# Softmax maxima over partitions in a graph attention kernel: from TensorE transposes to VectorE block transposes

## The chip, the cores and the metric

The kernel runs on one core of one Trainium2 chip. The core has five engines that run their own instruction queues side by side and meet by semaphores: TensorE (PE, matrix products and transposes, results in PSUM), VectorE (DVE), ScalarE (ACT), GpSimd (POOL) and SyncE (SP, which issues most DMAs). The metric is the device time of one execution in microseconds; the number given for a kernel is the median of its runs.

## The reference

The input is x of 3327 rows and 512 columns, and adj, a 3327 x 3327 matrix of zeros and ones. Two graph attention layers come first, then a layer norm, then a layer with signs and a second layer norm:

```python
def _gat_layer(x, W, adj):
    proj = x @ W
    Wh, Ws = jnp.split(proj, 2, axis=-1)
    scores = Wh @ Ws.T
    a = jax.nn.softmax(scores, axis=-1) * adj
    out = a @ Wh
    out = out + x
    return jax.nn.leaky_relu(out, NEG_SLOPE)
...
x = _layernorm(x + gat2(x, adj), axis=-1)
bw = sign(weight); ba = maximum(sign(x), 0)
x = _layernorm(x + relu(adj @ (ba @ bw.T)), axis=-1)
```

The change touches the softmax alone: each row of scores needs its maximum, which is subtracted before the exponential.

## The kernel before

The kernel works in 26 tiles of 128 rows. For each of the two attention layers (`attention(l, att)`) the scores are made transposed: the keys j lie on the 128 partitions, and the query rows i along the free axis. So the softmax's maximum over j is a maximum over partitions and over tiles. The rows i are taken in halves of 256 (`g`, 13 of them) and in chunks `c` of two halves (7 chunks; the last, c=6, has one half). `q` runs over 13 pairs of key tiles.

The products use a seven-product scheme (Strassen's, in Winograd's form) on 128x256 f32 blocks. For one (c, q), `scores` issues in two steps: the products z1, x2, z6, y5 in the first, z7, y3, z4 in the second. They accumulate in three PSUM banks, Z, X and Y (pool `ps_ch`). ScalarE copies p1, u2, p5, u3 and c21 out of them (L599, L634), VectorE adds c11 (`add11`, L609), c22 (`add22`, L624) and c12 (`add12`, L630). A bank is used again as soon as it is read out: the next z1 goes into the bank that `add11` has emptied, the next x2 into the one that `add12` has emptied.

`maximum` (L652) folds the scores of each q into `top[g]`, an array of 128 partitions x 2 x 256. After the last q of a chunk, `column_max` makes from it `off[g]`, in which every partition holds the maxima of the 256 columns. Its three parts are placed in one step: `fold` at -0.04 (takes the maximum of the two 256-wide parts of `top`), `across` at 0.36, `back` at 0.9. The numbers are places in the order of the step: all work of one step is sorted by its number, and each engine takes its instructions in that order.

The step loop (L976 to L1019) is one hand-written order for all engines. In step v it issues, for the half and q of number v+3, `shift` (0.0, subtract `off`, L727, VectorE) and `exponential` (0.12, L730, ScalarE); for number v+2 `running` (0.01, the sums, L738) and `masked` (0.4, times adj, L743, VectorE, followed by four sums on POOL, L781 to L784); in every second step, and in some more, `halved_sums` (0.6, L763, VectorE), `halved` (0.61, the casts L749 and L750, ScalarE) and `exact` (0.62, L772), with `keep_blocks` in the following step at 0.5: POOL stores the fp8 block `ab` to `adj_d` (L766). The tile `ab` has two buffers, so a third block waits for the landing of the store before last. For number v+30, counted in steps of `scores`, it issues the products of a later chunk, and `values` (L808) for number v. So `across` and `back` of chunk c are issued while the attention of chunk c-1 ends and the scores of chunk c+1 begin; the first `shift` that needs the new `off` is the first of the step after `back`.

`across` before: TensorE transposes 128x128 blocks of `top` into PSUM (`ptop`, L684, four a chunk), VectorE takes the row maxima (L687) and repeats them over 128 columns by multiplying a tile of ones (L689). `back` transposes these again (`poff`, L694), and VectorE copies the result to `off` (L698). Both PSUM tiles are of the pool `ps_tr`, which has one buffer that `finish` also uses (L848, L894, L904).

Of the kernel before, what the change touches and what calls it, by code (L numbers as in the profile page):

```python
# [9 lines left out]
F32 = mybir.dt.float32  # L10
# [5 lines left out]
ALU = mybir.AluOpType  # L16
AX = mybir.AxisListType
PSUM = bass.MemoryType.PSUM

P = 128  # L20
CT = 4
CW = CT * P
B = 32
HW = CW // 2
# [6 lines left out]
def kernel(  # L31
# [8 lines left out]
    nc = tc.nc  # L40
# [12 lines left out]
    def tiles_of(c):  # L53
        return range(c * CT, min(NT, (c + 1) * CT))

    def halves_of(c):
        return [g for g in (2 * c, 2 * c + 1) if g < NQ]
# [9 lines left out]
    keep = ctx.enter_context(tc.tile_pool(name="keep", bufs=1))  # L67
    ring = ctx.enter_context(tc.tile_pool(name="ring", bufs=2))
    ops = ctx.enter_context(tc.tile_pool(name="ops", bufs=2))
    small = ctx.enter_context(tc.tile_pool(name="small", bufs=4))  # L70
    ps_ch = ctx.enter_context(tc.tile_pool(name="ps_ch", bufs=3, space=PSUM))
    ps_acc = ctx.enter_context(tc.tile_pool(name="ps_acc", bufs=4, space=PSUM))
    ps_tr = ctx.enter_context(tc.tile_pool(name="ps_tr", bufs=1, space=PSUM))
# [7 lines left out]
    ident = keep.tile([P, P], F32, name="ident")  # L81
    make_identity(nc, ident)
    ident_h = keep.tile([P, P], BF16, name="ident_h")
    nc.vector.tensor_copy(ident_h, ident)
    ones = keep.tile([P, P], F32, name="ones")
    nc.vector.memset(ones, 1.0)
    eps = keep.tile([P, 1], F32, name="eps")
    nc.vector.memset(eps, EPS)
    mv = keep.tile([P, NT, 2], F32, name="mv")
# [461 lines left out]
    def attention(l, att):  # L551
# [5 lines left out]
        sc, top, total, off, adj, acc, gs, xs, ch = ({} for _ in range(9))  # L557
# [29 lines left out]
        def scores(c, q, s):  # L587
# [66 lines left out]
            if s == 1:  # L654

                after.append((-0.05, lambda: maximum(mine[0])))
                if q == NQ - 1:
                    after.extend(column_max(c))
# [8 lines left out]

        def column_max(c):

            n = len(tiles_of(c))  # L670
            mx = small.tile([P, CT], F32, tag="mx", name=f"mx_{l}_{c}")
            rep = [top[g][:, 1, ts(a, P)] for g in halves_of(c) for a in range(2)]

            def fold():
                for g in halves_of(c):
                    nc.vector.tensor_tensor(
                        top[g][:, 0], top[g][:, 0], top[g][:, 1], ALU.max
                    )

            def across():  # L680
                pt = ps_tr.tile([P, CT, P], F32, tag="tr", name=f"ptop_{l}_{c}")
                for i, g in enumerate(halves_of(c)):
                    for a in range(2):
                        nc.tensor.transpose(  # L684
                            pt[:, 2 * i + a, :], top[g][:, 0, ts(a, P)], ident
                        )
                nc.vector.reduce_max(mx[:, :n], pt[:, :n, :], axis=AX.X)  # L687
                for a in range(n):
                    nc.vector.tensor_scalar(rep[a], ones, mx[:, a : a + 1], None, ALU.mult)  # L689

            def back():
                pb = ps_tr.tile([P, CW], F32, tag="tr", name=f"poff_{l}_{c}")
                for a in range(n):
                    nc.tensor.transpose(pb[:, ts(a, P)], rep[a], ident)  # L694
                for i, g in enumerate(halves_of(c)):
                    off[g] = att.tile([P, 1, HW], F32, tag=f"off{i}", bufs=1,
                                      name=f"off_{l}_{g}")
                    nc.vector.tensor_copy(off[g][:, 0], pb[:, ts(i, HW)])  # L698

            return [(-0.04, fold), (0.36, across), (0.9, back)]  # L700

        def load_adj(g, q):
# [235 lines left out]
        else:  # L938
# [16 lines left out]
            n = len(steps) - end - 2  # L955
# [11 lines left out]
        mine = [i for i, e in enumerate(steps) if e[1] % L == l]  # L967
# [8 lines left out]
        for v in range(-LOOK - 4, len(steps)):  # L976
            u = v + LOOK
# [7 lines left out]
            for lead, load in ((2, load_xs), (4, load_gs)):  # L985
                if 0 <= u + lead < len(ahead):
                    c, q, h = ahead[u + lead]
# [23 lines left out]
            if last and 0 <= v - first_products < EARLY:  # L1011
                p = v - first_products
# [314 lines left out]
```

## Time and profile before

| what | value |
|---|---|
| median of 3 runs | 2633.66 us (2631.25 to 2634.98) |
| profiled execution | 2629.29 us |
| its span in the trace | 2627.5 us |
| mean granted TensorE clock | 0.998 |
| first and last `fold` (L676) | 267.7 and 2418.7 us |
| `fold`, 26 instructions | 10.0 us busy, 421 ns each |
| `shift` (L727), 338 instructions | 247.1 us busy, 731 ns each |
| `masked` (L743), 338 instructions | 237.5 us busy, 703 ns each |
| POOL waiting at L781 for L743 | 720.1 us in 260 waits |
| ScalarE's exponential waiting for L727 | 362.5 us in 218 waits |
| HBM traffic over the span | 242 GB/s |

The profile is of one execution. "Busy" is the time in which an engine's instructions overlap the clock, a share of the span; TensorE's instructions overlap each other, so their spacing says more than their own lengths. In a group's line, "idle before" is how long the engine stood still just before the instructions of that group, and after the arrow stands who ended that. There are 14 places at which `column_max` runs, 7 a layer, about 155 us apart in the middle of a layer: near 268, 416, 575, 734, 894, 1052 and 1177 us in layer 0, and 1487, 1636, 1800, 1964, 2127, 2291 and 2419 us in layer 1. Before the first of each layer there are no `values` yet, so TensorE does scores alone; after the last there are no scores any more.

### The profile page before, as it was taken

The page shows a single profiled execution, that of the slowest core. Times are in us where ns is not written, and L with a number is a line of the kernel's source. Part 1 is how long each engine was busy: PE and PEld are TensorE (multiplying, and loading weights), DVE is VectorE, ACT ScalarE, POOL GpSimd, SP SyncE. Part 2 cuts the span into 40 slices and gives each one's busy share as a digit, 9 for nine tenths or more (in the row PEclk, how much of TensorE's full clock was granted, in tenths as well). Part 3 has the DMA queues.
Part 4 walks back from the last instruction along what each step waited for, and adds up shares of the span by engine and source line. Part 5 has one row for each costly group of instructions (what it writes and reads, how often), then busy time and mean ns, then how long its engine had stood idle before and what let it go on. Part 6 is the DMA issues. An engine that isn't in the chain of part 4 may idle for free. (4 is left out here: it accounts for less than half of the span.)

```text
span 2627.5 us, 40294 instructions
## 1 busy us (share of the span) xinstructions
PE 2594.9 (99%) x12656; PEld 2249.1 (86%) x12656; DVE 2089.6 (80%) x4279; ACT 788.1 (30%) x1954; POOL 1098.4 (42%) x2025
## 2 busy tenths in 40 slices
PE   9999999999999999999999999999999999999998
PEld 6888888888888888887888888888888888888787
DVE  5864888889898886677875689888898888767976
ACT  2323332333333332222232333333333333222143
POOL 2640344444444444546552134444444444455510
PEclk9999999999999999999999999999999999999999
DMA  6855777787777776797865678777777777677775
GB/s 202 297 196 177 241 239 266 239 275 253 264 243 244 263 245 222 237 256 243 295 235 182 226 229 277 248 236 266 240 275 249 236 267 238 223 262 257 265 246 176
DMA packets 308055, 639.17 MB, mean 243 GB/s; under 512 B 34855, under 2 KB 175745, under 8 KB 306298
## 3 DMA queue, kind: packets, MB, share of 16 engines
q1 hardware_dynamic: 272140, 530.29, 61.9%
q0 software_dynamic: 35664, 106.18, 11.0%
q8 instruction: 104, 1.70, 0.3%
q14 instruction: 117, 0.96, 0.1%
q10 hardware_dynamic: 30, 0.03, 0.0%
HBM read 529.69 MB, written 106.67 MB: 242 GB/s over the span
## 5 line engine op out<-in xcount | busy, mean ns | idle before, releaser
L582 PE MATMUL pZ<-gs,xs 128*128 128x256 f32 x2496 | 636.0, 379 | 1.3 <-ACT u L599 1.3
L781 POOL TENSOR_TENSOR as<-s 128x128 f32<-128x128 f32 x338 | 162.4, 480 | 1048.1 <-DVE s L743 720.1
L582 PEld LDWEIGHTS pZ<-gs,xs 128*128 128x128 f32 x2496 | 473.5, 190 | 66.7 <-ACT u L599 2.4
L808 PE MATMUL acc<-ws,s 128*128 128x256 f32 x1352 | 402.2, 379 | 0.0
L808 PE MATMUL acc<-wh,s 128*128 128x256 f32 x1352 | 355.7, 379 | 0.6 <-DVE s L743 0.4
L808 PE MATMUL acc<-ws,as 128*128 128x256 f32 x1352 | 349.8, 380 | 3.9 <-POOL as L783 3.6
L730 ACT ACTIVATE s<-s 128x512 f32<-128x512 f32 x338 | 213.4, 631 | 362.8 <-DVE s L727 362.5
L582 PE MATMUL pY<-gs,xs 128*128 128x256 f32 x1248 | 320.8, 379 | 1.4 <-ACT p L599 1.4
L808 PEld LDWEIGHTS acc<-ws,as 128*128 128x128 f32 x1352 | 255.1, 190 | 44.6 <-POOL as L783 5.7
L808 PEld LDWEIGHTS acc<-wh,s 128*128 128x128 f32 x1352 | 256.6, 190 | 36.3 <-DVE s L743 1.5
L808 PEld LDWEIGHTS acc<-ws,s 128*128 128x128 f32 x1352 | 255.1, 190 | 33.9
L652 DVE TENSOR_TENSOR top<-top,s 128x512 f32<-128x512 f32 x312 | 223.7, 730 | 71.6 <-ACT s L639 51.8
L582 PEld LDWEIGHTS pY<-gs,xs 128*128 128x128 f32 x1248 | 236.6, 190 | 35.4 <-ACT p L599 3.3
L727 DVE TENSOR_TENSOR s<-s,off 128x512 f32<-128x512 f32 x338 | 247.1, 731 | 0.1
L743 DVE TENSOR_TENSOR s<-s,adj 128x512 f32<-128x512 f32 x338 | 237.5, 703 | 9.5 <-DMA adj<-in_adjT_dram 0.7
L738 DVE TENSOR_TENSOR total<-total,s 128x512 f32<-128x512 f32 x312 | 232.3, 745 | 0.0
L599 ACT COPY u<-pZ 128x256 f32<-128x256 f32 x312 | 115.8, 371 | 347.2 <-PE pZ L582 345.6
L783 POOL TENSOR_TENSOR as<-s 128x128 f32<-128x128 f32 x338 | 207.5, 614 | 26.5
L808 PE MATMUL acc<-wh,as 128*128 128x256 f32 x676 | 202.5, 381 | 0.0
L782 POOL TENSOR_TENSOR s<-s 128x128 f32<-128x128 f32 x338 | 184.9, 547 | 27.4
L784 POOL TENSOR_TENSOR as<-s,as 128x128 f32<-128x128 f32 x338 | 181.0, 535 | 26.5
L624 DVE TENSOR_TENSOR s<-p,u 128x256 f32<-128x256 f32 x156 | 66.7, 428 | 145.8 <-ACT u L599 144.8
(220 smaller groups left out, 3866.0 us busy)
## 6 DMA issues: line engine op xcount, KB each, us to landing
ws<-ws_d SPq DMA_DIRECT2D x338, 512.0 KB, 3.8
xs<-xs_d SPq DMA_DIRECT2D x182, 512.0 KB, 5.7
adj<-in_adjT_dram SPq DMA_DIRECT2D x324, 256.0 KB, 4.3
xs<-xs_d SPq DMA_DIRECT2D x156, 384.0 KB, 6.2
gs_d<-gsp POOLq DMA_DIRECT2D x88, 256.0 KB, 2.9
gs<-gs_d SPq DMA_DIRECT2D x12, 1792.0 KB, 10.4
adj_d<-ab POOLq DMA_DIRECT2D x169, 112.0 KB, 4.1
ahl<-adj_d SPq DMA_DIRECT2D x78, 224.0 KB, 4.9
```

Of the source, the lines that this page charges most:

```text
L582: nc.tensor.matmul(ch[bank], xs[c, q, a][:, k], gs[c][:, b, k], start=(start and k == 0), stop=(k == 1), skip_group_check=True,)
L599: nc.scalar.copy(ch[name], ch[bank])
L652: nc.vector.tensor_tensor(top[i], top[i], t, ALU.max)
L727: nc.vector.tensor_tensor(s, s, off[g].to_broadcast([P, 2, HW]), ALU.subtract)
L730: nc.scalar.activation(sc[g, q], sc[g, q], AF.Exp)
L738: nc.vector.tensor_tensor(total[g], total[g], sc[g, q], ALU.add)
L743: nc.vector.tensor_tensor(s, s, adj[g, q], ALU.mult)
L781: nc.gpsimd.tensor_tensor(s3, a11, a21, ALU.subtract)
L782: nc.gpsimd.tensor_tensor(a21, a21, a22, ALU.add)
L783: nc.gpsimd.tensor_tensor(s2, a21, a11, ALU.subtract)
L784: nc.gpsimd.tensor_tensor(s4, a12, s2, ALU.subtract)
L808: nc.tensor.matmul(acc[g][i // 2][:, i % 2], a[i], b[i], start=(q == 0 and i % 2 == 0), stop=(q == NQ - 1), skip_group_check=True,)
```

## The change

TensorE no longer takes part in `column_max`. `across` transposes 32x32 blocks of `top[g][:, 0]` into `top[g][:, 1]` on VectorE, takes the maxima of each block's rows (8 numbers a partition for a half), copies those of the four quadrants of 32 partitions side by side onto the first 32 partitions, takes the maximum of the four, and copies the result to the other three quadrants. `back` transposes blocks again, from an input in which each maximum is repeated 32 times by a stride of zero, straight into `off`. The tile `ones`, the PSUM tiles `ptop` and `poff` and their copies go; three small tiles with one buffer each come. `fold` stays, and so do the places of the three parts in the step.

```diff
-    ones = keep.tile([P, P], F32, name="ones")
-    nc.vector.memset(ones, 1.0)
...
         def column_max(c):
-            n = len(tiles_of(c))
-            mx = small.tile([P, CT], F32, tag="mx", name=f"mx_{l}_{c}")
-            rep = [top[g][:, 1, ts(a, P)] for g in halves_of(c) for a in range(2)]
+            mine = halves_of(c)
+            n = len(mine) * HW // B
+            part = small.tile([P, CW // B], F32, tag="mxq", bufs=1, name=f"mxq_{l}_{c}")
+            quad = small.tile([P, P // B, CW // B], F32, tag="mx4", bufs=1,
+                              name=f"mx4_{l}_{c}")
+            whole = small.tile([P, CW // B], F32, tag="mx", bufs=1, name=f"mx_{l}_{c}")
...
             def across():
-                pt = ps_tr.tile([P, CT, P], F32, tag="tr", name=f"ptop_{l}_{c}")
-                for i, g in enumerate(halves_of(c)):
-                    for a in range(2):
-                        nc.tensor.transpose(
-                            pt[:, 2 * i + a, :], top[g][:, 0, ts(a, P)], ident
-                        )
-                nc.vector.reduce_max(mx[:, :n], pt[:, :n, :], axis=AX.X)
-                for a in range(n):
-                    nc.vector.tensor_scalar(rep[a], ones, mx[:, a : a + 1], None, ALU.mult)
+                w = HW // B
+                for i, g in enumerate(mine):
+                    nc.vector.transpose(top[g][:, 1], top[g][:, 0])
+                    nc.vector.reduce_max(
+                        part[:, ts(i, w)],
+                        top[g][:, 1].rearrange("p (r u) -> p r u", u=B), axis=AX.X,
+                    )
+                for a in range(P // B):
+                    nc.vector.tensor_copy(quad[:B, a, :n], part[ts(a, B), :n])
+                nc.vector.reduce_max(
+                    whole[:B, :n], quad[:B, :, :n].rearrange("p a r -> p r a"), axis=AX.X
+                )
+                for a in range(1, P // B):
+                    nc.vector.tensor_copy(whole[ts(a, B), :n], whole[:B, :n])
 
             def back():
-                pb = ps_tr.tile([P, CW], F32, tag="tr", name=f"poff_{l}_{c}")
-                for a in range(n):
-                    nc.tensor.transpose(pb[:, ts(a, P)], rep[a], ident)
-                for i, g in enumerate(halves_of(c)):
+                w = HW // B
+                for i, g in enumerate(mine):
                     off[g] = att.tile([P, 1, HW], F32, tag=f"off{i}", bufs=1,
                                       name=f"off_{l}_{g}")
-                    nc.vector.tensor_copy(off[g][:, 0], pb[:, ts(i, HW)])
+                    nc.vector.transpose(
+                        off[g][:, 0].rearrange("p (r u) -> p r u", u=B),
+                        whole[:, ts(i, w)].unsqueeze(2).to_broadcast([P, w, B]),
+                    )
```

Here P is 128, B is 32, HW is 256 (a half) and CW is 512 (a chunk).

More of the change, by code (lines that the diff above doesn't have):

```diff
@@ L668, in column_max @@
         def column_max(c):
-            n = len(tiles_of(c))
-            mx = small.tile([P, CT], F32, tag="mx", name=f"mx_{l}_{c}")
-            rep = [top[g][:, 1, ts(a, P)] for g in halves_of(c) for a in range(2)]
+            mine = halves_of(c)
[4 more added lines that the diff above has]
+            whole = small.tile([P, CW // B], F32, tag="mx", bufs=1, name=f"mx_{l}_{c}")
             def fold():
-                for g in halves_of(c):
+                for g in mine:
                     nc.vector.tensor_tensor(
```

## The prediction

> **What bounds the kernel now.** I read the page's shares first, then the group table by tile shape, then the timeline around the places where the maxima are made, then the waits.
>
> The busy shares (page, part 1):
>
> ```profile
> PE 2594.9 (99%) x12656; PEld 2249.1 (86%) x12656; DVE 2089.6 (80%) x4279; ACT 788.1 (30%) x1954; POOL 1098.4 (42%) x2025
> ```
>
> TensorE is never free for long. Starts of 128x256 f32 matmuls follow each other at 0.216 us throughout the trace, so what leaves TensorE's queue shortens the run, unless something else is late instead. The groups that the change takes away or resembles (two answers of the group table, for TensorE and for VectorE; busy us, mean ns, idle before):
>
> ```profile
> L684 PE MATMUL ptop<-ident,top 128*128 128x128 f32 x52 | 8.7, 284 | 1.3 <-DVE top L676 1.1
> L694 PE MATMUL poff<-ident,top 128*128 128x128 f32 x52 | 8.1, 276 | 0.4 <-ACT baT L898 0.4
> ...
> L340 DVE STREAM_TRANSPOSE xT<-xr 128x512 f32<-128x512 f32 x44 | 47.9, 1096 | 0.0
> L689 DVE TENSOR_SCALAR top<-ones,mx 128x128 f32<-128x128 f32 x52 | 11.5, 283 | 0.5
> L857 DVE TENSOR_REDUCE rz<-pz 128x2 f32<-128x256 f32 x26 | 10.8, 415 | 4.9 <-PE pz L856 4.9
> L698 DVE COPY off<-poff 128x256 f32<-128x256 f32 x26 | 9.8, 414 | 3.4 <-PE poff L694 3.4
> L687 DVE TENSOR_REDUCE mx<-ptop 128x4 f32<-128x512 f32 x12 | 8.2, 685 | 2.2 <-PE ptop L684 2.2
> L262 DVE STREAM_TRANSPOSE wTs<-wl 128x128 f32<-128x128 f32 x32 | 7.0, 276 | 0.0
> ```
>
> See 104 TensorE transposes, and two VectorE transposes with a price by size: 276 ns at 128 elements a row, 1096 ns at 512, about 2.14 ns an element.
>
> One boundary, chunk 3 of layer 0 (timeline; start us, length):
>
> ```profile
> 734.58 0.68 PE L684 MATMUL ptop<-ident,top 128*128 128x128 f32 x4
> 735.10 0.60 PE L808 MATMUL acc<-ws,as 128*128 128x256 f32 x2
> 735.89 0.68 DVE L687 TENSOR_REDUCE mx<-ptop 128x4 f32<-128x512 f32 x1
> 736.61 0.88 DVE L689 TENSOR_SCALAR top<-ones,mx 128x128 f32<-128x128 f32 x4
> 737.40 0.68 DVE L743 TENSOR_TENSOR s<-s,adj 128x512 f32<-128x512 f32 x1
> 738.12 0.60 PE L694 MATMUL poff<-ident,top 128*128 128x128 f32 x4
> 738.56 0.60 PE L808 MATMUL acc<-ws,s 128*128 128x256 f32 x2
> 740.90 0.74 DVE L698 COPY off<-poff 128x256 f32<-128x256 f32 x2
> 741.57 0.67 DVE L727 TENSOR_TENSOR s<-s,off 128x512 f32<-128x512 f32 x1
> 743.71 0.41 DVE L630 TENSOR_TENSOR s<-pY,u 128x256 f32<-128x256 f32 x1
> 746.14 0.56 POOL L766 DMA_DIRECT2D adj_d<-ab  x1
> 746.33 1.03 PE L582 MATMUL pX<-gs,xs 128*128 128x256 f32 x4
> 752.54 0.41 ACT L749 CAST ab<-adj 128x256 fp8e4<-128x256 f32 x1 [2.99 <-DMA adj_d<-ab]
> 753.47 1.13 PE L582 MATMUL pY<-gs,xs 128*128 128x256 f32 x4 [0.50 <-ACT p L599]
> ```
>
> Four transposes take 0.52 and 0.44 us of TensorE (start to the next instruction's start). VectorE gives 1.51 us to `across` (735.89 to 737.40) and 0.67 to `back`. From 720 to 749 the same timeline has VectorE without a pause. Two later deadlines show: `pX` may start only when L630 has emptied the score bank it takes (744.12; it starts 2.21 us after that), and the `pY` product stalls because a ScalarE copy stands behind a cast that waits for the landing of an `adj_d` store.
>
> **What the Trainium skill says.** "VectorE: DVE Perf Modes", The three transpose paths: VectorE transposes only within 32x32 blocks, so partitions in different quadrants must be brought together separately; L340 and L262 are such transposes, and the trace has their price. The same page, The perf-mode tier table: tensor_reduce has no faster mode; the trace agrees, 415 ns at 256 and 685 ns at 512 elements, that is 1.05 ns an element and 0.15 us fixed. The same page, Two Vector instructions with no wait between them: an instruction whose input or output starts in another quadrant than that of the one before is held until that one has finished; no row of this trace shows such copies.
>
> **The change part by part.**
>
> TensorE. 52+52 transposes go. I add, over the 28 places, the time from the first transpose to the next other instruction, and the extra gap before it: L684 and L694 occupy 12.3 us at about 0.11 us each, and gaps of 2.95 us before them go too (0.74 and 0.65 at the two chunks 0, where TensorE waits for `fold`; 0.35 and 0.41 at 2293 and 2421). Together 15.2 us: 1.69 at each chunk 0, 1.21 and 0.95 at chunks 1 and 3 of layer 0, 9.7 at all the others. That is the ceiling.
>
> VectorE, a full chunk of two halves. `across`: a transpose of 256 elements is 0.55 us (2.14 ns x 256, from L340 and L262); a reduction of 256 is 0.42 (L857; its source is PSUM there and SBUF now, same size). Transpose and reduction, twice, each reduction after its transpose: 0.58 + 0.35 + 0.58 + 0.45 = 1.95 us. Four quadrant copies, 32 partitions x 16: not in the trace. From below 0.06 us (a 128x1 memset), from above 0.28 (L689, 128x128); I take 0.165, which is the fixed 0.15 and a little, and no overlap, as the held rule has it: 0.7. The reduction of 64 elements: 0.15 + 0.07 + 0.03 = 0.25. Three copies: 0.5. So 3.4 against 1.51. `back`: two transposes from a repeated input, 0.48 + 0.58 = 1.06 against 0.67 (I take the repeated read at the plain price). Added: 1.9 + 0.4 = 2.3 us a full chunk, bounds 1.4 to 3.2. Half chunks (c=6) add about 1.3. The waits of VectorE for `ptop` and `poff` (5.6 us in all) go, which pays part of it in chunks 0, 2, 4, 5 and 6. The memset of `ones` (0.17 us, at the start beside loads) is nothing, and the freed PSUM tag only removes waits already counted.
>
> What stands behind this VectorE work: `masked` is queued behind `across` and feeds POOL's four sums and then the `adj_d` store in POOL's queue; the next `shift` is behind `back`, ScalarE's exponential waits for it, and bank copies stand behind that; L609 and L630 empty the banks that the next `pZ` and `pX` take. So I compare a relative slip (VectorE later by 2.3, less waits saved, and TensorE earlier by what it saves) with the spare time between L630's end and the next `pX`:
> - chunks 1 to 4 of layer 1, 2 and 4 of layer 0: spare 3.36 to 4.09 us; slip 2.5 to 3.5. Hidden, but for some 0.3 us together. If the cover went, each would cost the excess one for one.
> - chunks 5: no full product follows. Gain kept. Chunks 6: VectorE has 1.9 us idle 8 us later in layer 1, which hides the slip. Gain kept. With the six above: -9.7 + 0.3 = -9.4.
> - chunk 0, both layers: spare 1.10 us. Placing the instructions one after the other (fold ends 268.44, `across` 271.75, L609 272.15, `back` 273.2, shift 273.9, L624 and L630 274.7), `pX` starts at 274.75, where it started at 274.39. The copies behind the two late exponentials add about 0.4. So +0.75 each instead of -1.69: +1.5.
> - chunks 1 and 3 of layer 0: spare 2.2; slip 3.3. `pX` comes out where it was. Then the `adj_d` store, issued at 746.14 after POOL's sums, is issued up to 2.3 us later; its landing (752.48, 6.3 us after issue) releases the cast, the copy and the stalled `pY`. I take +1.7 of 0 to 2.5 each, since part of those 6.3 us may be other traffic: +3.4.
>
> Sum: -9.4 + 1.5 + 3.4 = -4.5 us. The span 2627.5 becomes 2623.0, and the profiled execution of 2629.29 becomes 2624.8. The median of the runs, 2633.66, is 4.4 us above the profiled one; moved by the same amount it becomes 2629.2.
>
> **Rivals.**
> - The slip is hidden everywhere (small copies near 0.06 us, landings set by other traffic). For: VectorE is idle for 20% of the span, and only 14 spots are touched. Against: no pause around chunks 1 and 3. Then 11 to 15 us go: 2621.
> - Gain and loss cancel: the store's landing slips fully, and 1 us is lost at a few spots with spare 3.4. Then within 2 us of before: 2633.
> - Slower: the small copies cost some 0.35 us each, or the transposes of the repeated row are dear. Place: the 14 boundaries. Added VectorE work of 3.8 us in place of 2.3 uses up the spare of 3.4 to 4.1: the six good chunks gain nothing, each chunk 0 costs 2.3, chunks 1 and 3 of layer 0 3.2 each through the store, and only chunks 5 and 6 still gain 3: +8, 2642. It decides from about 3 us added. For: VectorE is busy for 11.69 of the 12 us from 731 to 743. Against: tiny instructions here (128x1 TENSOR_SCALAR) last 153 ns.
> - That the change doesn't do what it says: the same maximum per column is subtracted, so nothing else changes; I give it nothing.
>
> **How the numbers follow.** Forecast 0.53, hidden everywhere 0.2, cancel 0.1, slower 0.17. About 0.2%, 5.3 us, is what a measurement of this kernel tells from no change. The forecast's own range is 2625 to 2632, so half of it counts as faster. Faster 0.26 + 0.2 = 0.46; same 0.27 + 0.1 = 0.37; slower 0.17. The range goes from the hidden case's near end, 2621, to the middle of the way into the slower one, 2639.
>
> **What would show it.** In the changed kernel's profile: no `ptop` or `poff`; TensorE's stalls at the chunks 0 between L609 or L630 and `pZ` or `pX`, about 2 us each; the stall of `pY` 12 us after chunks 1 and 3 grown from 0.66 to 2 to 3 us; no new stall after layer 1's chunks 1 to 4; the seven copies near 0.165 us, the four transposes near 0.55. The prediction is wrong if stalls appear after layer 1's chunks, if the copies are far from 0.165, or if the stores' landings move with the other traffic rather than with their issue.

## The result, and the profile after

The changed kernel's median is 2628.43 us (2625.09 to 2631.35, 22 runs), against 2631.93 us for the kernel before on the same chips (2628.19 to 2635.05, 22 runs): a ratio of 0.9987, with a 95% interval of 0.9981 to 0.9993. That is 3.5 us less; 4.5 had been forecast. So of the 15.2 us that TensorE no longer spends at these places, about a quarter shows in the time.

The page of the changed kernel, its shares:

```profile
PE 2582.4 (98%) x12552; PEld 2238.6 (85%) x12552; DVE 2116.0 (81%) x4376; ACT 785.9 (30%) x1954; POOL 1104.1 (42%) x2025
```

TensorE is busy for 12.5 us less than before with 104 fewer matrix instructions; VectorE is busy for 26.4 us more. What the new VectorE work costs, from the group table (busy us, mean ns, idle before):

```profile
L686 DVE STREAM_TRANSPOSE top<-top 128x256 f32<-128x256 f32 x26 | 11.3, 437 | 0.0
L687 DVE TENSOR_REDUCE mxq<-top 128x8 f32<-128x256 f32 x26 | 10.9, 420 | 0.9
L704 DVE STREAM_TRANSPOSE off<-mx 128x256 f32<-128x256 f32 x26 | 10.0, 418 | 0.0
L692 DVE COPY mx<-mxq 32x16 f32<-32x16 f32 x48 | 7.8, 163 | 0.9
L697 DVE COPY mx<-mx 32x16 f32<-32x16 f32 x36 | 6.0, 166 | 0.7
```

The small copies take what was assumed. The transposes take less than the 550 ns assumed.

The same boundary as in the prediction, chunk 3 of layer 0 (timeline; start us, length; what it waited for):

```profile
735.99 0.44 DVE L686 STREAM_TRANSPOSE top<-top 128x256 f32<-128x256 f32 x1
...
737.72 0.69 DVE L692 COPY mx<-mxq 32x16 f32<-32x16 f32 x4
738.45 0.25 DVE L693 TENSOR_REDUCE mx<-mx 32x16 f32<-32x64 f32 x1
...
739.29 0.69 DVE L752 TENSOR_TENSOR s<-s,adj 128x512 f32<-128x512 f32 x1
...
742.78 0.76 DVE L704 STREAM_TRANSPOSE off<-mx 128x256 f32<-128x256 f32 x2
743.47 0.64 DVE L736 TENSOR_TENSOR s<-s,off 128x512 f32<-128x512 f32 x1
...
745.58 0.41 DVE L628 TENSOR_TENSOR s<-pY,u 128x256 f32<-128x256 f32 x1
...
746.05 1.13 PE L580 MATMUL pX<-gs,xs 128*128 128x256 f32 x4 [0.71 <-DVE s L628]
```

`across` occupies VectorE for 3.30 us (735.99 to 739.29) against 1.51 before, and `back` 0.69 against 0.67. The next `pX` now waits for VectorE to empty its bank (L628 here, L630 before), where it had 2.2 us to spare.

What TensorE waits for in the changed kernel (table of waits; us in total, times, longest):

```profile
PE acc L817 <- issue: 4.0, 3, 1.7
...
PE pX L580 <- DVE s L628: 3.5, 4, 1.2
...
PE pz L865 <- POOL adj L716: 2.7, 1, 2.7
...
PE pm L289 <- DVE wTs L260: 2.0, 1, 2.0
```

These four are new or have grown; in the kernel before, the table has 0.7 us for `pz`, none of the other three, and 1.1 us for `ptop`, which is gone. "Issue" at L817 is a wait that the table can't name. It falls at the change from one half to the next:

```profile
594.40 0.42 DVE L628 TENSOR_TENSOR s<-pY,u 128x256 f32<-128x256 f32 x1
...
595.79 0.51 DVE L772 TENSOR_TENSOR ab<-adj 128x128 fp8e4<-128x128 f32 x1 [0.98 <-DMA adj_d<-ab]
...
599.96 0.42 DVE L844 TENSOR_TENSOR ou<-acc,ou 128x256 f32<-128x256 f32 x1
...
600.48 1.10 PE L817 MATMUL acc<-ws,as 128*128 128x256 f32 x4 [1.56 <-issue]
```

This is 20 us after chunk 2 (timeline). The products of the new half go into the accumulator bank that L844 reads out, and start 0.10 us after L844 ends at 600.38. The same place in the kernel before:

```profile
595.48 0.42 DVE L630 TENSOR_TENSOR s<-pY,u 128x256 f32<-128x256 f32 x1
...
600.68 1.10 PE L808 MATMUL acc<-ws,as 128*128 128x256 f32 x4
```

There the same instruction of VectorE (L835) ended at 600.57. TensorE now comes to this meeting some 1.5 us earlier, VectorE just as late as before, and so nothing is gained.

VectorE was not late all along. At 594.40 it is 1.08 us ahead of the kernel before (L628 against L630). Then it stands still for 0.98 us, until the store to `adj_d` has landed whose buffer L772 takes. Without that, an estimate from these numbers, TensorE would have stood still for 0.6 us and not for 1.56. POOL issued that store at 591.35, where it had issued it at 590.75. Chunk 4 goes the same way. VectorE is 0.95 us ahead (913.05 against 914.00), then stands still for 1.42 us. The timeline puts this wait down to POOL's L792, but L772 reads nothing of it, and ScalarE's cast into the same buffer starts within 0.01 us of L772. The store was issued at 910.01 in place of 909.32, and TensorE then waits 1.70 us for its accumulator. So VectorE's added work can act through POOL as well: POOL's sums wait for `masked`, and the store stands behind them. That this is why the two stores were late was not tested.

Where the time went can be read from the start of the first `fold` of each chunk in the two timelines. The last column is the chunk's own share: the difference at the next `fold`, less that at this one. At the first `fold` the changed kernel is 1.2 us ahead already; that part of the trace has nothing of the change but the memset of `ones`, and over all traces here the first `fold` lies anywhere between 265.6 and 268.8 us.

| chunk | before, us | after, us | ahead (-) or behind | share of the chunk |
|---|---|---|---|---|
| layer 0, c=0 | 267.68 | 266.46 | -1.22 | +0.41 |
| 1 | 415.46 | 414.65 | -0.81 | +0.17 |
| 2 | 574.80 | 574.16 | -0.64 | +0.74 |
| 3 | 734.01 | 734.11 | +0.10 | -0.94 |
| 4 | 893.65 | 892.81 | -0.84 | +1.06 |
| 5 | 1051.06 | 1051.28 | +0.22 | -0.15 |
| 6, to layer 1's first | 1176.03 | 1176.10 | +0.07 | +1.33 |
| layer 1, c=0 | 1486.98 | 1488.38 | +1.40 | -0.23 |
| 1 | 1635.96 | 1637.13 | +1.17 | -1.27 |
| 2 | 1797.80 | 1797.70 | -0.10 | -0.81 |
| 3 | 1963.42 | 1962.51 | -0.91 | -0.66 |
| 4 | 2125.51 | 2123.94 | -1.57 | -0.45 |
| 5 | 2289.43 | 2287.41 | -2.02 | -1.29 |
| 6, to the end | 2418.70 | 2415.39 | -3.31 | +0.90 |

Layer 0 loses 2.6 us, layer 1 wins 3.8. VectorE is busy for 88% of the time in the middle of both (300 to 1050 and 1520 to 2290 us), so its idle time does not tell them apart. The waits for stores do: in the changed kernel L772 stands still for landings of `adj_d` for 13.6 us between 270 and 1180 us, and for 3.7 between 1480 and 2420. Whether that is the reason was not tested. The two last chunks, after which no scores follow, lose 2.2 us together.

### The profile page after: what moved, and what is told of

It is laid out like the page before. It is cut to its first block, busy times and chain, and to the rows that moved or that the text cites. A ratio compares the mean times of both kernels' runs of the same rounds, so it can differ in the third digit from the quotient of the medians.

```text
span 2625.1 us, 40169 instructions
## 1 busy us (share of the span) xinstructions
PE 2582.4 (98%) x12552; PEld 2238.6 (85%) x12552; DVE 2116.0 (81%) x4376; ACT 785.9 (30%) x1954; POOL 1104.1 (42%) x2025
## 5 line engine op out<-in xcount | busy, mean ns | idle before, releaser
L817 PE MATMUL acc<-ws,s 128*128 128x256 f32 x1352 | 402.2, 379 | 0.0
L817 PE MATMUL acc<-wh,s 128*128 128x256 f32 x1352 | 355.7, 379 | 0.6 <-DVE s L752 0.4
L817 PE MATMUL acc<-ws,as 128*128 128x256 f32 x1352 | 348.0, 380 | 7.0 <-issue 4.0
L817 PEld LDWEIGHTS acc<-ws,as 128*128 128x128 f32 x1352 | 255.9, 190 | 48.8 <-issue 8.9
L817 PEld LDWEIGHTS acc<-wh,s 128*128 128x128 f32 x1352 | 256.7, 190 | 36.2 <-DVE s L752 1.4
L817 PEld LDWEIGHTS acc<-ws,s 128*128 128x128 f32 x1352 | 256.0, 190 | 34.5
L792 POOL TENSOR_TENSOR as<-s 128x128 f32<-128x128 f32 x338 | 208.6, 617 | 26.5
L817 PE MATMUL acc<-wh,as 128*128 128x256 f32 x676 | 202.5, 381 | 0.0
```

The lines of the kernel that those rows point to most:

```text
L792: nc.gpsimd.tensor_tensor(s2, a21, a11, ALU.subtract)
L817: nc.tensor.matmul(acc[g][i // 2][:, i % 2], a[i], b[i], start=(q == 0 and i % 2 == 0), stop=(q == NQ - 1), skip_group_check=True,)
```

## The experiments

All ratios are to the kernel before, run on the same chip, with 95% intervals. The runs are called e1 to e12, by the first part of their labels. Two theories stood against each other. The first: TensorE's release is worth its full 15 us, and VectorE's longer work gives most of it back by being late for TensorE. The second: TensorE is held anyway by other meetings with VectorE and by the stores to `adj_d`, so that the release was worth little, whatever VectorE does.

**No spread at all.** `across` is empty, and `back` copies each partition's own maxima.

```diff
             def across():
-                w = HW // B
-                for i, g in enumerate(mine):
-                    nc.vector.transpose(top[g][:, 1], top[g][:, 0])
...
+                pass
...
-                    nc.vector.transpose(
-                        off[g][:, 0].rearrange("p (r u) -> p r u", u=B),
-                        whole[:, ts(i, w)].unsqueeze(2).to_broadcast([P, w, B]),
-                    )
+                    nc.vector.tensor_copy(off[g][:, 0], top[g][:, 0])
```

> Leaves out the maximum over partitions and its spread: off is a copy of each partition's own maxima, so the output is another. Neither TensorE nor VectorE works on the spread; VectorE does about 1.8 us less per chunk than before and 3.6 us less than after. Theory (TensorE's 15.2 us are worth their full length, and VectorE's added work gave back about 11 of them): 13 to 18 us faster than before, ratio 0.993 to 0.995. Rival (TensorE is held by other meetings with VectorE and the adj_d stores that do not depend on these places): like the changed kernel, ratio 0.998 to 0.9995.

Measured (e1): 2611.66 us, ratio 0.9926 (0.9913 to 0.994), 19.4 us faster than before. The second theory falls: with both engines relieved, the full 15 us go, and more, so the meetings and stores that remain do not hold the kernel near its present time. VectorE is relieved here against the kernel before too (2068.6 us busy, 21.0 less), so the 19.4 us are not TensorE's alone.

**Only the quadrant step left out.** Block transposes and row maxima stay; the seven copies and the reduction of four go.

```diff
-                        part[:, ts(i, w)],
+                        whole[:, ts(i, w)],
...
-                for a in range(P // B):
-                    nc.vector.tensor_copy(quad[:B, a, :n], part[ts(a, B), :n])
-                nc.vector.reduce_max(
-                    whole[:B, :n], quad[:B, :, :n].rearrange("p a r -> p r a"), axis=AX.X
-                )
-                for a in range(1, P // B):
-                    nc.vector.tensor_copy(whole[ts(a, B), :n], whole[:B, :n])
```

> Leaves out the seven quadrant copies and the reduction of four, so each quadrant subtracts its own maximum and the output differs by that. VectorE's across falls from 3.3 to about 1.8 us, near the 1.5 us of before; no TensorE transposes. Theory (the loss is VectorE's length): 9 to 14 us faster than before, ratio 0.9945 to 0.9965. Rival (the length doesn't matter, only that VectorE now does it): like the changed kernel, 0.998 to 0.9995.

Measured (e2): 2616.21 us, ratio 0.9945 (0.9931 to 0.9958), 14.9 us faster than before. This is near the ceiling of 15.2 us that the prediction had summed up from the spacing of TensorE's instructions; the interval reaches from 11 to 18 us. VectorE is busy for 2095.1 us here, 20.9 less than in the changed kernel, and the run is 11.4 us shorter against before: 0.55 us for each us of VectorE's.

**The kernel before with VectorE filler.** Four block transposes more in `across`, ahead of the row maxima.

```diff
+                for g in halves_of(c):
+                    for _ in range(2):
+                        nc.vector.transpose(top[g][:, 1], top[g][:, 0])
                 nc.vector.reduce_max(mx[:, :n], pt[:, :n, :], axis=AX.X)
```

> The kernel before with four extra VectorE block transposes of 256 elements (two in the last chunk) in across, about 1.7 us a chunk, 22 us in all; TensorE's work unchanged. Theory: VectorE's lateness alone costs 5 to 11 us, ratio 1.002 to 1.004. Rival (hidden by VectorE's idle time): 0.9995 to 1.0005.

Measured (e3): 2644.94 us, ratio 1.0048 (1.0035 to 1.0062), 13.9 us slower, more than either theory said. The experiment was not clean, as the waits of TensorE in it show:

```profile
PE pbt L899 <- DVE mx L690: 4.0, 4, 1.2
...
PE poff L697 <- DVE top L692: 3.1, 6, 0.8
```

TensorE waits here for its own transposes' input, and for the PSUM buffer that the late row maxima (L690) hold. That is 7.1 us of the 13.9, and no part of the changed kernel. The wait of `pY` for ScalarE's copy grew too, from 1.4 to 4.9 us, and TensorE's clock fell to half twice, which the next run explains.

**The changed kernel with the same filler**, behind the last copy of `across`, where TensorE waits for it in no direct way.

```diff
                 for a in range(1, P // B):
                     nc.vector.tensor_copy(whole[ts(a, B), :n], whole[:B, :n])
+                for g in mine:
+                    for _ in range(2):
+                        nc.vector.transpose(top[g][:, 1], top[g][:, 0])
```

> The changed kernel with four extra VectorE block transposes (two in the last chunk) behind the last copy of across, about 1.7 us a chunk, 22 us in all; TensorE waits for none of them directly, as it did in e3. Theory (0.55 us per us): 12 us slower than the changed kernel, ratio to before 1.0025 to 1.0045. Rival (e3's cost was TensorE waiting for its own transposes' input): 0 to 5 us slower than the changed kernel, ratio 0.9987 to 1.0006.

Measured (e7): 2645.55 us, ratio 1.006 (1.0046 to 1.0073), some 19 us slower than the changed kernel for at most 22 us of VectorE. TensorE's waits have moved to these lines:

```profile
PE acc L820 <- issue: 7.9, 4, 2.7
PE pX L580 <- ACT s L632: 7.4, 4, 3.7
```

The second line is ScalarE. Its two long waits, 3.7 and 3.3 us, come after chunks 1 and 3 of layer 0. At chunk 3 the copy stands behind casts (L761, L762) that wait for the landing of a store to `adj_d`, the path that the prediction had followed there. At chunk 1 the timeline names a load of `adj` for the cast, while VectorE's work on the same buffer waits for such a store. After chunk 1, and after chunk 3:

```profile
435.07 1.54 PE L580 MATMUL pX<-gs,xs 128*128 128x256 f32 x4 [3.68 <-ACT s L632]
436.40 1.91 PE L820 MATMUL acc<-ws,as 128*128 128x256 f32 x4
...
758.96 0.41 ACT L761 CAST ab<-adj 128x256 fp8e4<-128x256 f32 x1 [1.37 <-DMA adj_d<-ab]
```

The line of L820 shows a second cost. Four such products take 1.03 us elsewhere and 1.91 here. The table of windows has TensorE's granted clock at half for this stretch (the numbers behind the engines' busy times are clock, DMA share and GB/s):

```profile
436.00:438.00 2.00, 2.00 (x6) 1.65 (x5) 2.00 (x6) 0.28 (x1) 0.00 (x0) 0.50 0.34 125
```

In windows of 0.1 us, such a spell at half clock lasts 3.4 us each time. The changed kernel's trace has one while it has work, near 1252 us, and so has the trace before. In e7 there are seven more, two of them in a row at 275 us, all at stalls of TensorE. One takes 1.7 us from a TensorE that is busy, so together up to 12 of the 22.4 us by which this trace is longer than the changed kernel's. The mean clock of the five executions is 0.993 to 0.995, against 0.996 to 0.998 in the changed kernel. What is left, some 10 us for 17.0 us more of busy VectorE, is about the price found by e2. So e7 does not show that the price of VectorE's time itself grows. It shows that TensorE's longer stalls can cost more than their length.

**TensorE's share put back.** The changed kernel with 104 TensorE transposes of the identity, which nobody reads, at the old places.

```diff
+                pt = ps_tr.tile([P, CT, P], F32, tag="tr", name=f"ptop_{l}_{c}")
+                for i in range(2 * len(mine)):
+                    nc.tensor.transpose(pt[:, i], ident, ident)
...
+                pb = ps_tr.tile([P, CT, P], F32, tag="tr", name=f"poff_{l}_{c}")
+                for i in range(2 * len(mine)):
+                    nc.tensor.transpose(pb[:, i], ident, ident)
```

> The changed kernel with 104 TensorE transposes of the identity that nobody reads, at the old places, about 11.4 us of TensorE; VectorE's work unchanged. Theory (TensorE sets the pace all the time and VectorE's lateness is paid on top): 9 to 13 us slower than the changed kernel, ratio to before 1.002 to 1.0037. Rival (around these places VectorE sets the pace, so TensorE's release was worth little): 1 to 6 us slower, ratio 0.999 to 1.001.

Measured (e8): 2633.38 us, ratio 1.001 (1.0002 to 1.0019), 6.4 us slower than the changed kernel for 11.4 us of TensorE's. It lies between the two expectations, at the upper edge of the rival's. The transposes put back read only the identity, so they wait for nothing: of the 15.2 us they bring back the work, but not the 2.95 us of gaps. Together with e2 it gives the table of the case, in us against before:

| | VectorE as long as before (about) | VectorE as in the change |
|---|---|---|
| TensorE's transposes there | 0 | +2.9 |
| TensorE's transposes gone | -14.9 | -3.5 |

With VectorE's long work, TensorE's release is worth 6.4 us; without it 14.9. With TensorE's transposes, VectorE's longer work costs 2.9 us; without them 11.4. Each ratio is known to some 1.5 to 3.5 us, and the missing gaps may make the 6.4 too small by up to 3; the two releases still differ. Neither engine's price stands alone: each is spare time for the other.

**`across` later in its step**, behind `masked`, `add11`, `halved_sums` and `exact`.

```diff
-            return [(-0.04, fold), (0.36, across), (0.9, back)]
+            return [(-0.04, fold), (0.63, across), (0.9, back)]
```

> The changed kernel with across at 0.63 in place of 0.36: behind masked, add11, halved_sums and exact of its step, just ahead of back. Same instructions. Theory A (what costs is the work queued behind across in its own step: masked, POOL's sums, the adj_d store): 2 to 6 us faster than the changed kernel, ratio to before 0.9965 to 0.998. Theory B (what costs is the next step's shift and what follows it, which come as late as ever): like the changed kernel, 0.998 to 0.9995.

Measured (e4): 2627.79 us, ratio 0.9989 (0.998 to 0.9997): no difference. The order inside the step is not what costs. That is as it must be if the work behind the step's end, which comes as late as ever, is what costs; the run doesn't show which part of that work counts.

**The last chunk of each layer on TensorE as before**, six chunks a layer on VectorE. Only the tile `ones` stays away: the row maxima are repeated by a copy from a stride of zero.

```diff
-                    after.extend(column_max(c))
+                    after.extend((column_max_pe if c == NC - 1 else column_max)(c))
```

> The changed kernel with the last chunk of each layer on TensorE as before. In the changed kernel's trace TensorE waits 2.0 us for wTs and 2.7 us for pz after these chunks, against 0.26 and 0.8 before. Theory: 2 to 4 us faster than the changed kernel, ratio to before 0.997 to 0.9982. Rival (those waits only move to the next meeting of the engines): like the changed kernel, 0.9982 to 0.9993.

Measured (e11): 2623.26 us, ratio 0.9967 (0.9955 to 0.9979), some 5 us faster than the changed kernel. In its table of waits `pm` behind `wTs` is gone, and `pz` is back at 0.6 us:

```profile
PE pz L899 <- POOL adj L750: 0.6, 1, 0.6
```

So two of the 14 places cost about 5 us, where the change gained 3.5 in all. The two waits were 4.1 us longer than here. A spell at half clock may be the rest: e4, which has the same instructions as the changed kernel, has one behind its wait of 2.14 us for `wTs`, and 18 of the 22 executions of the changed kernel had a mean clock of 0.997 or less, where all six of e11 had 0.998 or more.

**The quadrants brought together by POOL.** Six copies on POOL give every quadrant all four maxima, so that nothing is spread back; VectorE then reduces four columns in all partitions.

```diff
+                for x, y in ((0, 64), (64, 0)):
+                    nc.gpsimd.tensor_copy(quad[x : x + 64, 1, :n], quad[y : y + 64, 0, :n])
+                for x, y in ((0, 1), (1, 0), (2, 3), (3, 2)):
+                    nc.gpsimd.tensor_copy(quad[ts(x, B), 2:, :n], quad[ts(y, B), :2, :n])
...
             def back():
+                nc.vector.reduce_max(
+                    whole[:, :n], quad[:, :, :n].rearrange("p a r -> p r a"), axis=AX.X
+                )
```

> The changed kernel with the quadrants brought together by six copies on POOL (every quadrant gets all four, so nothing is spread back), and one VectorE reduction of 128x64 in back. VectorE's work per full chunk falls from 4.0 to about 2.7 us (17 us in all). Theory (about 0.55 us of time per us of VectorE work at these places, as the changed kernel and e2 differ): 9 us faster than the changed kernel, ratio to before 0.9945 to 0.9965. Rival (POOL's copies hold up its sums and the stores as much as VectorE did): like the changed kernel, 0.998 to 0.9995.

Measured (e5): 2621.93 us, ratio 0.9967 (0.9955 to 0.9979), 8.5 us faster than before, about 5 faster than the changed kernel where 9 were expected. VectorE is busy for 20 us less, but it now waits for POOL, 7.5 us at the full chunks (group table; the last number is the wait) and 1.7 at the last ones:

```profile
L697 DVE TENSOR_REDUCE mx<-mx 128x16 f32<-128x64 f32 x12 | 3.1, 259 | 7.5 <-POOL mx L693 7.5
```

**As that, with the two halves of a chunk in one tile**: one fold, one transpose and one reduction of 512.

```diff
-                for g in mine:
-                    nc.vector.tensor_tensor(top[g][:, 0], top[g][:, 0], top[g][:, 1], ALU.max)
+                nc.vector.tensor_tensor(all_[:, :m, 0], all_[:, :m, 0], all_[:, :m, 1], ALU.max)
...
+                nc.vector.transpose(all_[:, :m, 1], all_[:, :m, 0])
```

> As e5, with the two halves of a chunk in one tile: one fold, one block transpose and one reduction of 512 in place of two of 256 each, about 0.35 us less VectorE work a chunk (4 us in all). Theory: 2 us faster than e5, ratio to before 0.9938 to 0.996. Rival: nothing beyond e5.

Measured (e6): 2622.3 us, ratio 0.9965 (0.9952 to 0.9979): nothing beyond e5. VectorE's busy time fell by 2.2 us, not 4.

**As e5, with `across` at 0.005**, so that POOL's copies lie beside three more instructions of VectorE.

```diff
-            return [(-0.04, fold), (0.36, across), (0.9, back)]
+            return [(-0.04, fold), (0.005, across), (0.9, back)]
```

> As e5, with across at 0.005 in place of 0.36, so that POOL's six copies lie beside running, masked and add11; in e5 VectorE waits 9.2 us in all for them. Theory (VectorE time at these places is worth about half its length): 3 to 6 us faster than e5, ratio to before 0.994 to 0.9958. Rival (running and what follows come 1.7 us later in their step, which costs as much): like e5, 0.9962 to 0.9972.

Measured (e9): 2624.07 us, ratio 0.9974 (0.9964 to 0.9985), not faster than e5. VectorE still waits for POOL for 7.7 us (6.5 and 1.2). POOL's copies of 64 x 16 took 534 ns on average, where in e5 they took 329, so that the earlier start was partly used up. VectorE worked beside them in both, and why they were slower is not shown.

**Both with the last chunks on TensorE.** The edit is that of e11, made in e9 and in e5.

> As e9, with the last chunk of each layer (c=6) on TensorE as before (the row maxima repeated by a copy from a stride of zero instead of the tile of ones). Theory (after the last scores VectorE sets the pace, so its 1.1 us there cost in full and TensorE's 1 us cost nothing): 2 to 4 us faster than e9. Rival: no difference.

> e5 (quadrants joined by POOL, across at 0.36) with the last chunk of each layer on TensorE as before. If the two savings add (e5 5 us below the changed kernel, e11 5 us below it), 13 us faster than before, ratio 0.9942 to 0.996. If e5 already had most of what the last chunk gives, like e5, 0.996 to 0.9972.

Measured: 2618.99 us, ratio 0.9958 (0.9944 to 0.9971), for the first (e10); 2621.16 us, ratio 0.9963 (0.995 to 0.9977), for the second (e12). By the medians the two savings don't add; the interval of e12 covers both of its expectations, and those of e5, e10, e11 and e12 overlap. Of the kernels that leave nothing out, e10 has the best median, 11 us below the kernel before. The changed kernel's interval (0.9981 to 0.9993) lies above those of e5, e10, e11 and e12.

## Why the prediction was right

**The ceiling.** The sum of 15.2 us from spacing and gaps fits: e2, with VectorE about as long as before, gained 14.9.

**VectorE's added work.** 2.3 us a full chunk had been worked out; it is 1.8 (3.99 against 2.18). The seven copies were right at 0.165 us (measured 163 and 166 ns), with hardly any overlap: four take 0.69 us. Mis-sized were the transposes. The price of 2.14 ns an element from L340 and L262 was carried to rows in one piece, which take 437 and 418 ns at 256 elements, and 704 at 512 in e6. The line through L340 and L262 was the slip: L262's 276 ns at 128 elements lie near the new ones, and L340's 1096 ns at 512 lie far above. L340 reads single elements with a step, the new ones don't; that this is the reason was not tested.

**Chunks 0.** Foreseen +0.75 each, measured +0.41 and -0.23, with the stall of `pX` on VectorE that had been named, 0.79 us long where about 2 were foreseen. From `fold` to `pX` both chunks are 0.3 us shorter than before (6.4 against 6.7), where `pX` had been put 0.36 later. The transposes' price is part of that.

**Chunks 1 and 3 of layer 0.** The slip did catch `pX`, as said. The next step failed: that the `adj_d` store lands later by as much as it is issued later, +1.7 us each. At chunk 3 the store was issued at 748.01 in place of 746.14, and the fp8 work behind it began at 751.45 where it had begun at 752.50. The stall of `pY` 12 us after is gone. (At chunk 1 it is gone too, but a `pY` 44 us after the fold stalls for 1.21 us, where it had stalled for 0.20.) So the landing did not follow the issue here; that other traffic sets it, the alternative that the prediction had left open, would fit and was not tested. Measured: +0.17 and -0.94.

**Chunks 2 and 4 of layer 0, and chunks 6.** The steps that failed most. "Hidden" was concluded from the first deadline, `pX`, alone. TensorE, ahead by its gain, then met VectorE at the change of half, where before it had waited only 0.27 us: +0.74 and +1.06 where about -0.9 each had been put down. VectorE had been 1 us ahead there and lost it to the landing of a store issued 0.6 to 0.7 us later. That is the path that the prediction had followed at chunks 1 and 3, and had left out here. "Gain kept" for the last chunks rested on 1.9 us of VectorE's idle time 8 us later in layer 1. But layer 0's tail has TensorE waiting for `wTs` (2.0 us) behind the same VectorE queue, and layer 1's has it waiting for `pz` (2.7 us). e11 puts a price of about 5 us on these two places, against the gain of 1.5 us that the sum held. Chunk 5 of layer 0, also put down as kept, gained 0.15 us.

**Layer 1, chunks 1 to 5.** Foreseen about -5.5, measured -4.5. One new stall appeared, against the forecast: 0.72 us at the change of half behind chunk 3.

The total was close in good part by luck, because the errors were of both signs: the losses at chunks 0, 1 and 3 were smaller than thought, those at 2, 4 and 6 larger. The rival of full hiding falls, by e2 and e8. The rival "slower", which asked for 3 us and more of added VectorE work a chunk, was tried with the filler of e7: with 1.8 + 1.7 us added a chunk the kernel is slower than before by 15 us, 0.6%. The rival had put 8 us on 3.8 added; it did not foresee the half clock.

What stays open: how the 11.4 us that VectorE gave back divide among bank, accumulator, store and ScalarE waits, and how much of them is clock (its mean is 0.998 or 0.999 in all five executions of e2, and 0.997 in most of the changed kernel's). e4 shows only that the order within the step doesn't matter, and the single trace's shares add up to 1.2 us of gain where the medians show 3.5.

## What to carry to other kernels

When work moves from the engine that sets the pace to one at 80%, don't price the two sides one by one: here the release was worth 14.9 us or about 6.4, and the added work 2.9 or 11.4, according to what the other engine did. A slip that the first deadline hides is not hidden: follow the late queue to every later meeting with the bounding engine, through stores and their buffers too, above all to the changes of accumulator and the ends of stages, which cost most here. And look at the granted clock of short stretches before you read a longer time as the price of the work added. A cheap repair here was to leave the old way in the few places where the relieved engine has time.

## What the runs showed of the hardware

A VectorE block transpose of 128x256 f32 from rows in one piece takes 437 ns, and 418 from an input repeated by a stride of zero. At 512 elements the instruction of e6 takes 704 ns, and L340, which reads with a step, 1096. A VectorE copy of 32 partitions x 16 takes 163 ns. On POOL a copy of 32 partitions x 32 f32 takes 219 ns and one of 64 x 16 takes 329 ns on average (e5), so that six of them are slower than VectorE's seven; in e9 those of 64 x 16 took 534.

At some stalls of TensorE its granted clock fell to half for 3.4 us: in e7 at stalls of 2.7 to 3.7 us, in e3 at 2.3 and 2.7, in e4 at 2.1, and at 275 us in e7 for twice that, after 1.7 and 0.8 us close together. At others it did not: 2.73 us at 935 in e7, 2.69 at 2434 in the changed kernel. What decides it, these runs don't show.
